# Later scans' inputs in another order over two PSUM banks, and the expert sort in a bank of its own

## The chip, the cores and the metric

The kernel runs on one core of a Trainium2 chip. The core has five engines, each with a queue of its own that it works off in order: PE (TensorE, matrix products; PEld is its weight load), DVE (VectorE), ACT (ScalarE), POOL (GpSimd) and SP (SyncE, which here only starts transfers). They wait for each other by semaphores. PE writes into PSUM[...]. The metric is the device time of one execution in microseconds (us), as the median of several runs; less is better.

## The reference

Two layers over x of 4 batches x 1024 tokens x 128 features. Each layer modulates by a conditioning vector, normalises, mixes tokens, and then applies a routed mixture of experts:

```python
h = layernorm(x) * (1 + ca) + sa
x = x + ga * L0_attention(h)          # 16 heads, 4 key heads, rotary, causal
h = layernorm(x) * (1 + cb) + sb
x = x + gb * L0_ffn(h)                # 8 experts, two best of each token, gated by silu
h = layernorm(x) * (1 + ca) + sa
x = x + ga * L1_mamba(h)              # convolution, selective scan with 16 states
h = layernorm(x) * (1 + cb) + sb
x = x + gb * L1_moe(h)                # 8 experts with a capacity, two best of each token
```

The selective scan is, for every feature and state, h = exp(delta * A) * h + delta * B * u along the tokens, with output y = sum over states of h * C, plus D * u; u is silu of a short causal convolution, delta is softplus of a projection of u, B and C are projections of u, and y is multiplied by silu(z).

## The kernel before

**Layer 0.** Attention runs batch by batch in two passes each. Beside it, in single steps that a Python generator yields, run the parts of other batches: `sort_tokens(b)` (L364) routes the tokens of batch b to layer 0's experts, and `Blocks` (L426 on) computes the experts in blocks of 128 rows. Batch 3's sort, its blocks and the return of its rows (`first_returns`) lie in layer 1's scans.

**The sort.** `sort_tokens` normalises (`norm_steps`), transposes (`feature_steps`, `tp`), makes router logits `fpl`, finds the two best experts (`top2_steps`), and counts in one PSUM tile `fpin`, by matrix products, how many earlier tokens go to each expert. `find_blocks` and `f_pos` (L404) read these counts in PSUM. At the end GpSimd starts 16 indirect transfers `blocks_in` (L418), which put the rows in the order of the experts. All its PSUM tiles have the tag "m".

**Layer 1's scans.** A batch has 32 scans: two halves of 512 tokens by 16 chunks of 8 features x 16 states. For each, `scan` (L988) lets PE spread `du` into PSUM (`pu`), DVE multiply it by `bb` (L997), ACT make the decay `da` by exp (L999), DVE run the scan `h` (L1001) and POOL multiply by `cc` (L1005, `hc`). PE sums groups of four `hc` into `py` (`collected`), and after each half `scan_output` gates it (`yh`), projects it (`pw`), gates again (`wide_gated`, L1023) and POOL adds it to x (L1025).

**The inputs of a batch's scans** come from `scan_inputs(b)` (L923): normalised x (`xn`), transposed (`hT`); for each half the convolution (`xc`, L967) and z (`sz`, L970), both with silu; `delta_steps` (L266) projects `pd`, copies it to `sp_r` and runs softplus (`sp_e` with exp on ACT, then the chain of L249 to L263 on DVE); `spread_delta` makes `dg` (L933) from it; `made_of` (L925) makes `dt` by ones x `dg`, and `bb` and `cc` by projections of `xc`, each in a PSUM bank of 512 columns that ACT copies out (L928). `du` (L977) is the product of `dt` and `xc` on POOL. The inputs of batch 0 (b == 0) use the two banks "m" and "d"; those of the later ones only "m".

**PSUM in layer 1:** four banks for `pu`, one for `py`, one "g" (in the scans of batch 1 used by the first layer's blocks), one "m", and one "d" (for `pw` and the routing `dispatch`).

**What sets the order.** The loop over batches (L1275 on) takes steps of the generators after each pair of scans: in batch 0 the return of layer 0's rows, the sort of batch 3 (four steps a pair), `shift_and_scale` and the inputs of batch 1 (two steps a pair); in later ones `dispatch` of the batch before and the inputs of the next. This program order isn't the order on the chip: a planner at build time puts each instruction into its engine's queue when its operands and its buffer come free by the planner's own reckoning, earlier program order first. A tile that waits for a bank thus moves back in its queue, and others move ahead of it.

Of the kernel before, what the change touches and what calls it, by code (L numbers as in the profile page):

```python
# [11 lines left out]
F32 = mybir.dt.float32  # L12
# [6 lines left out]
P = 128  # L19
# [30 lines left out]
def adaln_two_layers(ctx: ExitStack, tc: tile.TileContext, I: dict, out: bass.AP):  # L50
# [14 lines left out]
    def load(pool, name, eng=nc.sync):  # L65
# [6 lines left out]
    make_identity(nc, ident)  # L72
    ones = cst.tile([P, P], F32, name="ones")
    nc.gpsimd.memset(ones, 1.0)

    causal = cst.tile([P, P], F32, name="causal")
    nc.gpsimd.memset(causal, 0.0)
    nc.gpsimd.affine_select(
        out=causal, in_=causal, compare_op=ALU.is_ge, fill=NEG, base=0, pattern=[[-1, P]], channel_multiplier=1
    )  # L80

    before = cst.tile([P, P], F32, name="before")
    nc.gpsimd.affine_select(
# [277 lines left out]
        nc.vector.tensor_reduce(which, past, AX.X, ALU.add)  # L361
        return blocks, upto, which

    def sort_tokens(b, kept, pool, ps, hpool, tag, xtag="fxn"):  # L364


        xn = pool.tile([P, TB, D], F32, tag=xtag, bufs=1, name="fxn")
        yield from norm_steps(b * TB, TB, xn)
        hT = hpool.tile([P, S], F32, tag=tag, bufs=1, name="fhT")
        yield from feature_steps(xn, hT, ps, modT[0][:, 4, b : b + 1], modT[0][:, 3, b : b + 1])  # L370
        pl = ps.tile([P, TB, NE], F32, tag="m", name="fpl")
        for t in range(TB):
            mm(nc, pl[:, t, :], hT[:, t * P : (t + 1) * P], f_gate)
        yield
        m1, m2, oh1, oh2 = yield from top2_steps(pl, sm)

        both = sm.tile([P, TB, NE], F32, tag="f_both", bufs=1, name="f_both")
        nc.vector.tensor_add(both, oh1, oh2)
        flat = both.rearrange("p t e -> p (t e)")
        pin = ps.tile([P, TB + 1, NE], F32, tag="m", name="fpin")  # L380
        pinf = pin.rearrange("p t e -> p (t e)")
        mm(nc, pinf[:, : TB * NE], before, flat, stop=False)
        for n in range(1, TB):
            mm(nc, pinf[:, n * NE : TB * NE], ones, flat[:, : (TB - n) * NE], start=False, stop=(n == TB - 1))
        mine = sm.tile([P, NE], F32, tag="f_mine", bufs=1, name="f_mine")
        nc.vector.tensor_reduce(mine, both.rearrange("p t e -> p e t"), AX.X, ALU.add)
        mm(nc, pin[:, TB, :], ones, mine)
        yield
        z = sm.tile([P, TB], F32, tag="f_z", bufs=1, name="f_z")
        nc.vector.scalar_tensor_tensor(z, m1, 1e-20, m2, ALU.add, ALU.add)  # L390
        nc.vector.reciprocal(z, z)
        w = keep.tile([P, 2, TB], F32, tag=f"f_w{b}", name="f_w")
        nc.vector.tensor_mul(w[:, 0], m1, z)
        nc.vector.tensor_mul(w[:, 1], m2, z)
        yield

        blocks, upto, which = yield from find_blocks(pin[:, TB, :], NB, sm)
        expert = keep.tile([P, NB], I32, tag=f"f_expert{b}", name="f_expert")
        nc.vector.tensor_scalar(expert, which, float(NE - 1), None, ALU.min)
        yield  # L400

        nc.vector.tensor_tensor(upto, upto, blocks, ALU.subtract)
        pos = sm.tile([P, TB, NE], F32, tag="f_pos", bufs=1, name="f_pos")
        nc.vector.scalar_tensor_tensor(  # L404
            pos, upto.unsqueeze(1).to_broadcast([P, TB, NE]), float(P), pin[:, :TB, :], ALU.mult, ALU.add
        )
        yield
        place = sm.tile([P, 2, TB], F32, tag="f_place", bufs=1, name="f_place")
        placei = keep.tile([P, 2, TB], I32, tag=f"f_placei{b}", name="f_placei")
        for k, oh in enumerate((oh1, oh2)):  # L410
            nc.vector.tensor_mul(oh, oh, pos)
            nc.vector.tensor_reduce(place[:, k], oh, AX.X, ALU.add)
            yield
        nc.vector.tensor_copy(placei, place)
        kept[b] = expert, placei, w
        for t in range(TB):
            for k in range(2):
                nc.gpsimd.indirect_dma_start(  # L418
                    out=f_in[b][:, :],
                    out_offset=bass.IndirectOffsetOnAxis(ap=placei[:, k, t : t + 1], axis=0),  # L420
                    in_=xn[:, t, :],
                    in_offset=None,
                )
                yield
# [71 lines left out]
    with ExitStack() as es:  # L496
# [21 lines left out]


        MW = 512 + QG  # L520
        mask = aw.tile([P, MW], F32, name="mask")
        nc.gpsimd.memset(mask, 0.0)
        for j in range(4):
# [329 lines left out]
    with ExitStack() as es:  # L853
# [68 lines left out]

        def scan_inputs(b):  # L923

            def made_of(g, to, w, of):  # L925
                bank = ps_m.tile([P, 512], F32, tag=next(tags), name="p1")
                mm(nc, bank, w, of)
                nc.scalar.copy(to[:, half_of(g)], bank)  # L928

# [8 lines left out]
            dt, du, bb, cc = (wide(name) for name in ("dt", "du", "bb", "cc"))  # L938
            if b == 0:
                xc, sz, dl = first_made  # L940
                tags = itertools.cycle(("m", "d"))
                dg = spread_delta(dl)

                for g in range(2):
                    tok = half_of(g)
                    made_of(g, dt, ones, dg[g])
                    nc.gpsimd.tensor_mul(du[:, tok], dt[:, tok], xc[:, tok])
                    made_of(g, bb, m_B, xc[:, tok])
                    made_of(g, cc, m_C, xc[:, tok])
                return sz, xc, dt, du, bb, cc  # L950
            tags = itertools.repeat("m")
            xn = mb.tile([P, TB, D], F32, tag="xn", bufs=1, name="xn")
            yield from norm_steps(b * TB, TB, xn)
            hT = wide("hT", 1, S + 3)
# [6 lines left out]
                xc, sz = wide("xc", 1), wide("sz", 1)  # L961
            for g in range(2):
                tok = half_of(g)
                p1 = ps_m.tile([P, 512], F32, tag="m", name="p1")
                for k in range(4):
                    mm(nc, p1, conv_in[:, k, :], hT[:, tok.start + k : tok.stop + k], start=(k == 0), stop=(k == 3))
                nc.scalar.activation(xc[:, tok], p1, AF.Silu, bias=m_cb)  # L967
                p2 = ps_m.tile([P, 512], F32, tag="m", name="p2")
                mm(nc, p2, m_in[:, D:], hT[:, tok.start + 3 : tok.stop + 3])
                nc.scalar.activation(sz[:, tok], p2, AF.Silu)  # L970
                yield
            dl = yield from delta_steps(xc, ps_m)
            dg = spread_delta(dl)
            yield
            for g in range(2):
                made_of(g, dt, ones, dg[g])
            nc.gpsimd.tensor_mul(du, dt, xc)  # L977
            yield

            for to, w in ((bb, m_B), (cc, m_C)):  # L980
                for g in range(2):
                    made_of(g, to, w, xc[:, half_of(g)])
                yield
            return sz, xc, dt, du, bb, cc

        turn = itertools.count()
# [288 lines left out]
        for b in range(B):  # L1275
# [2 lines left out]
            beside, among = [], []  # L1278
            if b == 0:
                beside.append(Beside(first_returns(B - 2, db, 6), 4, 1))  # L1280
                beside.append(Beside(sort_tokens(B - 1, kept, db, ps_m, db, "hT2", "hx"), 2, 4))
                beside.append(Beside(shift_and_scale(), NCH - 3, 1))
            if b == 1:
                among.append(Beside(first_blocks(B - 1), 1, 1))
# [238 lines left out]
```

## Time and profile before

| | |
|---|---|
| median of 3 runs | 2082.4 us (2079.97 to 2082.79) |
| the profiled execution | 2072.22 us |
| its span, first to last instruction | 2070.5 us |
| PE busy | 1779.8 us (86%) |
| DVE busy | 1331.4 us (64%) |
| ACT busy | 944.8 us (46%) |
| POOL busy | 1000.4 us (48%) |
| scans of batch 0 | 1415.1 to 1499.3 us |
| scans of batch 1 | 1530.8 to 1627.4 us |
| scans of batch 2 | 1634.9 to 1742.9 us |
| scans of batch 3 | 1771.0 to 1848.5 us |
| first matrix product of layer 1's experts | 1884.2 us |

The profile is of one execution. A row of its timeline gives start, length, engine, line of the kernel, operation, the tile written and the tiles read, their shapes, and in square brackets how long the engine was idle before and what ended that. `hc<-h,cc` means that `hc` is made of `h` and `cc`. A share of busy time over the whole span mixes attention, scans and experts, which have different limits, so it is read by stretches.

### The profile page before, as it was taken

How to read it: one execution, taken by the hardware profiler on the slowest of the kernel's cores; microseconds unless marked ns; L12 is line 12 of the kernel's file. 1: busy time of each engine (PE TensorE's matmuls, PEld its weight loads, DVE VectorE, ACT ScalarE, POOL GpSimd, SP SyncE). 2: the span in 40 equal slices, each digit the busy share in tenths (PEclk: the TensorE clock that was granted, in tenths of full speed). 3: DMA queues.
4: the chain of work that ended last, by engine and by line, in shares of the span. 5: the costliest groups of instructions: out<-in, count | busy, mean ns of one | idle time of the engine just before them, and what ended most of it. 6: DMA issues, size and time to landing. Idle time of an engine off the chain costs nothing. (4 is left out here: it accounts for less than half of the span.)

```text
span 2070.5 us, 29042 instructions
## 1 busy us (share of the span) xinstructions
PE 1779.8 (86%) x8957; PEld 964.2 (47%) x8957; DVE 1331.4 (64%) x4005; ACT 944.8 (46%) x2071; POOL 1000.4 (48%) x1282
## 2 busy tenths in 40 slices
PE   5999899898999899899989899997779757757994
PEld 2444454453555345455535445553335423325774
DVE  5666556665667666566766566567858887782144
ACT  2364453743455374355455445455556345422321
POOL 3345335446333634633363653227654775773145
PEclk8899999999999999999999999998879887967997
DMA  6502002002222201212210122111003230002255
GB/s 202 186 1 52 1 1 52 1 26 63 64 64 78 56 1 32 78 54 71 78 40 1 48 68 68 51 43 38 31 27 111 76 108 13 8 20 83 80 156 177
DMA packets 104332, 124.63 MB, mean 60 GB/s; under 512 B 15088, under 2 KB 68720, under 8 KB 104176
## 3 DMA queue, kind: packets, MB, share of 16 engines
q1 hardware_dynamic: 83872, 98.75, 15.9%
q0 software_dynamic: 8192, 16.74, 2.7%
q10 hardware_dynamic: 12112, 7.29, 1.2%
q8 instruction: 71, 1.16, 0.2%
q14 instruction: 85, 0.70, 0.1%
HBM read 68.38 MB, written 33.42 MB: 49 GB/s over the span
## 5 line engine op out<-in xcount | busy, mean ns | idle before, releaser
L663 POOL TENSOR_SCALAR pr<-pr,den 128x32 f32<-128x32 f32 (+31 forms) x512 | 356.2, 711 | 308.2 <-DVE den L660 300.2
L657 ACT ACTIVATE pr<-pr,nb 128x32 f32<-128x32 f32 (+31 forms) x512 | 371.7, 727 | 164.5 <-DVE nb L644 158.5
L672 PE MATMUL pt<-ident,pr 128*128 128x128 f32 x2304 | 342.2, 283 | 47.2 <-POOL pr L663 37.2
L672 PEld LDWEIGHTS pt<-ident,pr 128*128 128x128 f32 x2304 | 253.9, 142 | 242.5 <-POOL pr L663 78.1
L46 PE MATMUL sc<-k,q 64*128 64x512 f32 (+14 forms) x1536 | 333.6, 527 | 33.6 <-DVE nb L644 25.5
L46 PE MATMUL po<-pT,v 128*64 128x512 f32 x1152 | 342.6, 621 | 2.8 <-DVE pT L676 2.8
L674 ACT COPY pT<-pt 128x512 f32<-128x512 f32 x288 | 167.5, 582 | 353.9 <-PE pt L672 302.5
L644 DVE CUSTOM_DVE_ANT_0 pr<-sc,mask 128x512 f32<-128x512 f32 (+15 forms) x512 | 272.8, 559 | 67.4 <-PE sc L46 57.0
L676 DVE COPY pT<-pt 128x512 f32<-128x512 f32 x288 | 198.2, 688 | 159.4 <-PE pt L672 145.9
L46 PEld LDWEIGHTS sc<-k,q 64*128 64x128 f32 x1536 | 125.4, 195 | 186.9 <-DVE nb L644 88.6
L1005 POOL TENSOR_TENSOR hc<-h,cc 128x512 f32<-128x512 f32 x128 | 161.7, 1276 | 87.7 <-DVE h L1001 32.2
L46 PE MATMUL pu<-du,spread 128*128 128x512 f32 x256 | 149.6, 694 | 54.5 <-DVE h L1001 43.5
L793 POOL MEMSET pr<- 128x288 f32 x128 | 42.4, 340 | 245.8 <-PE pt L672 241.6
L644 DVE CUSTOM_DVE_ANT_0 pr<-sc,mask,nb 128x416 f32<-128x416 f32 (+15 forms) x256 | 120.0, 496 | 7.3 <-PE sc L46 6.2
L999 ACT ACTIVATE da<-dt,negA 128x512 f32<-128x512 f32 x128 | 91.4, 718 | 62.7 <-DVE h L1001 62.3
L46 PEld LDWEIGHTS po<-pT,v 128*64 128x64 f32 x1152 | 68.9, 135 | 84.0 <-issue 41.4
L46 PEld LDWEIGHTS pu<-du,spread 128*128 128x128 f32 x256 | 47.6, 213 | 128.4 <-DVE h L1001 74.6
L1391 POOL DMA_INDIRECT y<-slots_out,slot x56 | 56.6, 1010 | 88.4 <-PE ph L46 52.1
L613 POOL TENSOR_TENSOR q<-rot_u,rot_v 128x512 f32<-128x512 f32 x64 | 81.3, 1272 | 36.4 <-DMA rot_v<-rot_w 35.3
L997 DVE TENSOR_TENSOR pu<-pu,bb 128x512 f32<-128x512 f32 x128 | 85.1, 684 | 18.0 <-PE pu L46 9.2
L657 ACT ACTIVATION_READ_ACCUMULATOR pr<-pr,nb 128x1 f32 x512 | 96.2, 188 | 0.0
L418 POOL DMA_INDIRECT blocks_in<-fxn,f_placei x64 | 64.6, 1009 | 57.3 <-DMA blocks_in<-fxn,f_placei 46.6
(281 smaller groups left out, 2695.3 us busy)
## 6 DMA issues: line engine op xcount, KB each, us to landing
fw<-in_f_w SPq DMA_DIRECT2D x92, 320.0 KB, 2.9
rot_v<-rot_w SPq DMA_DIRECT2D x300, 64.0 KB, 2.0
gw<-in_g_w SPq DMA_DIRECT2D x15, 512.0 KB, 5.7
fxe<-blocks_in SPq DMA_DIRECT2D x28, 192.0 KB, 2.5
blocks_out<-fye SPq DMA_DIRECT2D x28, 192.0 KB, 2.8
blocks_in<-mask SPq DMA_DIRECT2D x20, 256.0 KB, 2.9
slots_in<-mask SPq DMA_DIRECT2D x16, 256.0 KB, 3.7
g_w<-in_g_w SPq DMA_DIRECT2D x8, 512.0 KB, 7.3
```

The costliest lines, as they stand in the source:

```text
L46: return nc.tensor.matmul(out, lhsT, rhs, start=start, stop=stop)
L418: nc.gpsimd.indirect_dma_start(out=f_in[b][:, :], out_offset=bass.IndirectOffsetOnAxis(ap=placei[:, k, t : t + 1], axis=0), in_=xn[:, t, : ...
L613: nc.gpsimd.tensor_add(to, u.rearrange("p (n q) -> p n q", q=QG), v.rearrange("p (n q) -> p n q", q=QG))
L644: nc.vector.tensor_tensor_reduce(out=pr[hp][:, g, lo:hi], in0=sc[:, hp, : hi - lo], in1=mask[:, MW - hi + lo :] if hi == nk else mask[:, : ...
L657: nc.scalar.activation(p, p, AF.Exp, bias=nb[:, last, hp : hp + 1], scale=-1.0, accum_out=den[:, hp : hp + 1])
L663: nc.gpsimd.tensor_scalar(p, p, den[:, hp : hp + 1], 1.0, ALU.mult, ALU.mult)
L672: next_to(hp == 0 and g == 0, lambda: nc.tensor.transpose(to, p, ident))
L674: nc.scalar.copy(pT[:, hp, :], pt)
L676: nc.vector.tensor_copy(pT[:, hp, :], pt)
L997: nc.vector.tensor_mul(pu, pu, bb[:, tok])
L999: nc.scalar.activation(da, dt[:, tok], AF.Exp, scale=negA[:, c : c + 1])
L1005: nc.gpsimd.tensor_mul(hcs[-1], h, cc[:, tok])
```

## The change

- `scan_inputs` of batches 1 to 3 takes banks from `new_bank()`: alternately "m" and "g" for batches 1 and 3, only "m" for batch 2 (whose inputs are made in the scans of batch 1, when "g" holds blocks).
- In it the order is new: both convolutions; then `pd`; then both z; then softplus, with B beside its first part and C beside its second; then `dg`, `dt`, and `du` in two halves.
- The sort of batch 3 uses bank "d" in place of "m". In every sort the counts are copied from PSUM (`f_ahead`), and what follows reads the copy.
- The mask's `causal` pattern is a tile of attention's pool (tag "fam") in place of a constant of its own.

```diff
-    causal = cst.tile([P, P], F32, name="causal")
-    nc.gpsimd.memset(causal, 0.0)
-    nc.gpsimd.affine_select(
-        out=causal, in_=causal, compare_op=ALU.is_ge, fill=NEG, base=0, pattern=[[-1, P]], channel_multiplier=1
-    )
...
-    def sort_tokens(b, kept, pool, ps, hpool, tag, xtag="fxn"):
+    def sort_tokens(b, kept, pool, ps, hpool, tag, xtag="fxn", bank="m"):
...
-        yield from feature_steps(xn, hT, ps, modT[0][:, 4, b : b + 1], modT[0][:, 3, b : b + 1])
-        pl = ps.tile([P, TB, NE], F32, tag="m", name="fpl")
+        yield from feature_steps(xn, hT, ps, modT[0][:, 4, b : b + 1], modT[0][:, 3, b : b + 1], tag=bank)
+        pl = ps.tile([P, TB, NE], F32, tag=bank, name="fpl")
...
-        pin = ps.tile([P, TB + 1, NE], F32, tag="m", name="fpin")
+        pin = ps.tile([P, TB + 1, NE], F32, tag=bank, name="fpin")
...
         mm(nc, pin[:, TB, :], ones, mine)
+        ahead = sm.tile([P, TB + 1, NE], F32, tag="f_ahead", bufs=1, name="f_ahead")
+        nc.vector.tensor_copy(ahead, pin)
...
-        blocks, upto, which = yield from find_blocks(pin[:, TB, :], NB, sm)
+        blocks, upto, which = yield from find_blocks(ahead[:, TB, :], NB, sm)
...
-            pos, upto.unsqueeze(1).to_broadcast([P, TB, NE]), float(P), pin[:, :TB, :], ALU.mult, ALU.add
+            pos, upto.unsqueeze(1).to_broadcast([P, TB, NE]), float(P), ahead[:, :TB, :], ALU.mult, ALU.add
...
+        causal = ab.tile([P, P], F32, tag="fam", name="causal")
+        nc.gpsimd.memset(causal, 0.0)
+        nc.gpsimd.affine_select(
+            out=causal, in_=causal, compare_op=ALU.is_ge, fill=NEG, base=0, pattern=[[-1, P]], channel_multiplier=1
+        )
         mask = aw.tile([P, MW], F32, name="mask")
...
         def scan_inputs(b):
 
+            def new_bank():
+                pool, tag = next(tags)
+                return pool.tile([P, 512], F32, tag=tag, name="p1")
+
             def made_of(g, to, w, of):
-                bank = ps_m.tile([P, 512], F32, tag=next(tags), name="p1")
+                bank = new_bank()
...
-                tags = itertools.cycle(("m", "d"))
+                tags = itertools.cycle(((ps_m, "m"), (ps_m, "d")))
...
-            tags = itertools.repeat("m")
+
+            free = b != 2
+            tags = itertools.cycle(((ps_m, "m"), (ps_g, "g"))) if free else itertools.repeat((ps_m, "m"))
...
             for g in range(2):
                 tok = half_of(g)
-                p1 = ps_m.tile([P, 512], F32, tag="m", name="p1")
+                p1 = new_bank()
                 for k in range(4):
                     mm(nc, p1, conv_in[:, k, :], hT[:, tok.start + k : tok.stop + k], start=(k == 0), stop=(k == 3))
                 nc.scalar.activation(xc[:, tok], p1, AF.Silu, bias=m_cb)
-                p2 = ps_m.tile([P, 512], F32, tag="m", name="p2")
-                mm(nc, p2, m_in[:, D:], hT[:, tok.start + 3 : tok.stop + 3])
-                nc.scalar.activation(sz[:, tok], p2, AF.Silu)
                 yield
-            dl = yield from delta_steps(xc, ps_m)
-            dg = spread_delta(dl)
-            yield
+            delta = delta_steps(xc, ps_m)
+            next(delta)
             for g in range(2):
+                p2 = new_bank()
+                mm(nc, p2, m_in[:, D:], hT[:, g * 512 + 3 : g * 512 + 515])
+                nc.scalar.activation(sz[:, half_of(g)], p2, AF.Silu)
+            yield
+
+            try:
+                next(delta)
+                for g in range(2):
+                    made_of(g, bb, m_B, xc[:, half_of(g)])
+                yield
+                next(delta)
+                for g in range(2):
+                    made_of(g, cc, m_C, xc[:, half_of(g)])
+                yield
+                next(delta)
+                assert False
+            except StopIteration as end:
+                dg = spread_delta(end.value)
+            yield
+            for g in range(2):
+                tok = half_of(g)
                 made_of(g, dt, ones, dg[g])
-            nc.gpsimd.tensor_mul(du, dt, xc)
-            yield
-
-            for to, w in ((bb, m_B), (cc, m_C)):
-                for g in range(2):
-                    made_of(g, to, w, xc[:, half_of(g)])
-                yield
+                nc.gpsimd.tensor_mul(du[:, tok], dt[:, tok], xc[:, tok])
+            yield
             return sz, xc, dt, du, bb, cc
...
-                beside.append(Beside(sort_tokens(B - 1, kept, db, ps_m, db, "hT2", "hx"), 2, 4))
+                beside.append(Beside(sort_tokens(B - 1, kept, db, ps_m, db, "hT2", "hx", "d"), 2, 4))
```

## The prediction

> **What bounds the kernel now.** I read the page first (engine shares, slices, chain of waits), then cut the span into stretches at the starts and ends of the scans (L1001), the work of layer 1 that runs from 1415 to 1848 us. The reason for the cut: before it the slices show PE at 9 tenths in nearly every one, and the change touches next to nothing there; in the scans PE falls to 7 and the chain of waits is made of `DVE h L1001`, `POOL hc L1005` and `issue`. Each batch has 32 scans. The last of one batch and the first of the next bound a gap. The busy times of the stretches, in pairs of batch and gap (length; then busy us and instructions of PE, PEld, DVE, ACT, POOL; PE's granted clock; DMA share; GB/s):
>
> ```profile
> 1415.00:1499.30 84.30, 65.90 (x200) 27.14 (x198) 73.55 (x133) 46.26 (x84) 58.27 (x54) 0.84 0.08 26
> 1499.30:1530.80 31.50, 17.69 (x46) 7.93 (x47) 9.39 (x57) 14.46 (x24) 15.04 (x15) 0.57 0.06 19
> 1530.80:1627.40 96.60, 84.91 (x414) 48.08 (x412) 86.81 (x181) 55.96 (x105) 50.87 (x45) 0.98 0.27 81
> 1627.40:1634.90 7.50, 6.11 (x17) 3.56 (x18) 1.95 (x7) 1.28 (x2) 6.84 (x7) 0.60 0.12 33
> 1634.90:1742.90 108.00, 75.81 (x288) 35.63 (x286) 92.23 (x184) 48.12 (x92) 76.18 (x64) 0.83 0.22 75
> 1742.90:1771.00 28.10, 17.40 (x70) 10.08 (x71) 10.90 (x53) 14.03 (x25) 21.70 (x19) 0.74 0.11 33
> 1771.00:1848.50 77.50, 54.60 (x164) 18.47 (x162) 73.87 (x116) 30.34 (x59) 57.54 (x48) 0.83 0.04 12
> ```
>
> Inside a batch DVE is busy 85 to 95%: it bounds. In the three gaps (31.5 + 7.5 + 28.1 = 67.1 us) no engine is full: DVE does 9.4, 2.0 and 10.9 us. There a chain of dependences sets the time. The timeline of the first gap shows the chain:
>
> ```profile
> 1501.95 1.01 POOL L418 DMA_INDIRECT blocks_in<-fxn,f_placei  x1 [0.70 <-issue]
> 1502.99 1.27 POOL L1005 TENSOR_TENSOR hc<-h,cc 128x512 f32<-128x512 f32 x1
> 1504.32 1.93 PE L46 MATMUL py<-hc,gather 128*32 128x512 f32 x8 [6.37 <-POOL hc L1005]
> 1506.18 2.08 PE L46 MATMUL p<-hT,m_in_sb 128*128 128x512 f32 x2
> 1509.76 2.18 PE L46 MATMUL pd<-m_dt_sb,xc 128*128 128x1 f32 x16
> 1519.99 2.05 PE L46 MATMUL p<-dg,ones 128*128 128x512 f32 x2 [7.09 <-DVE dg L933]
> 1525.49 2.35 POOL L977 TENSOR_TENSOR du<-dt,xc 128x1024 f32<-128x1024 f32 x1 [4.79 <-ACT dt L928]
> 1530.81 1.22 DVE L1001 TENSOR_TENSOR_SCAN h<-da,pu 128x512 f32<-128x512 f32 x1
> ```
>
> The second z matrix and `pd` stand in PE's queue behind `py`, which waits for the last products `hc` on POOL, and those stand behind issues of `blocks_in`. Then softplus, `dg`, both `dt` and a `du` over both halves follow one after another through the one bank m.
>
> **The change, part by part.** The instructions' order of the changed kernel is known from its build, so I count in it.
>
> *Gap 0 to 1.* The sort of batch 3 no longer holds m, so `xn`, the convolutions, `pd`, B, C and `dt` all stand before the 29th scan of batch 0 in PE's and ACT's queues, both halves of `du` before hc 27 on POOL. Between the batches DVE has no instruction but pu (56 others before). Gap 31.5 to about 1.
>
> *Gap 1 to 2* (m only). `du` stands before the last two products, B and C are copied ahead; 6 other DVE instructions are left. 7.5 to about 2.
>
> *Gap 2 to 3.* Softplus still ends after the last scan; 27 DVE instructions against 52. POOL issues six `slots_in`, adds a gated x and only then makes `du`:
>
> ```profile
> 1744.68 1.02 POOL L1088 DMA_INDIRECT slots_in<-hs,desti  x1 [0.31 <-DVE rank L1083]
> 1746.02 1.00 POOL L1088 DMA_INDIRECT slots_in<-hs,desti  x1 [0.30 <-issue]
> 1747.32 0.97 POOL L1088 DMA_INDIRECT slots_in<-hs,desti  x1 [0.30 <-DMA slots_in<-hs,desti]
> ```
>
> The pitch is 1.29. POOL's leg: last hc 1.3 + 6 x 1.29 + x 1.3 + half of `du` 1.2 (2.35/2) + pu matmul 1.1 + pu product 0.7 = 13.3; I take 13.8 with semaphores. The other leg (hc 1.3, py 1.1, yh, nine softplus steps, `dg` 1.22, `dt` matmul and copy) ends near 9 and is hidden. Gain 14.3; bounds 8 and 18.
>
> Sum of the gaps: -30.5 - 5.5 - 14.3 = -50.3.
>
> *What comes back.* **DVE instructions that lay in a gap now lie among scans.** Counted by batch (all but pu and scan): 68, 117, 119, 51 before; 87, 144, 142, 55 after: 73 more, among them the softplus of batches 1 and 3 and layernorm statistics. In the first gap one cost 9.39/57 = 0.165 us. Beside `hc` on POOL it can cost more, as two steps of the same form in batch 1 show:
>
> ```profile
> 1607.54 1.19 DVE L257 SCALAR_TENSOR_TENSOR sp_s<-sp_s,sp_w 128x8 f32<-128x8 f32 x1
> 1609.25 0.15 DVE L257 SCALAR_TENSOR_TENSOR sp_s<-sp_s,sp_w 128x8 f32<-128x8 f32 x1
> ```
>
> The first began inside an `hc` (1607.43 to 1608.70). The Trainium skill, "SBUF — State Buffer", section "Who interferes with whom", gives a rule that speaks against this change: a DVE instruction with two SBUF inputs and a GpSimd one that reads SBUF share a port pair under an exclusive lock, and the later one blocks until the earlier ends. How often does it strike? Of the 359 such other instructions in the four batches, 34 lasted over 0.4 us longer than the shortest of their form, 35.1 us in all: 9.5%, 1.03 us each. So one costs 0.165 + 0.098 = 0.263, and 73 cost 19 us. If the lock struck each of them: 73 x 1.2 = 88 us. I take the measured share; bounds 12 and 45.
>
> **POOL.** The 16 `blocks_in` issues of batch 3's sort, ten of which lay in the gap, now lie between hc 19 of batch 0 and hc 6 of batch 1. An issue takes 0.98 and waits for the landing of the one before; alternating with one hc the pitch was 3.0 (1498.94, 1501.95). I laid out the queue: 16 issues, 18 hc, two halves of `du`, two adds of x, eight copies of `scb`: 53 us from about 1475 to 1528. DVE alone would be there at about 1520. Scans may run three buffers of `h` ahead of POOL, so 0 to 8 us; I take 5.
>
> **ACT.** Six table loads now stand within three scans (after `da` 21, 22 and 23) and `pu` 20 waits in PE's queue behind the first `pd`, which waits for ACT's first `xc`; scan 21 waits behind `sp_r` for the second.
>
> ```profile
> 1488.01 1.28 ACT L967 ACT_TABLE_LOAD   x1
> 1489.30 0.69 ACT L967 ACTIVATE xc<-p,m_cb_sb 128x512 f32<-128x512 f32 x1
> ```
>
> By the row six are 6 x 1.29 = 7.7 us. "ScalarE: Activation LUTs", "What ACT_TABLE_LOAD costs", adds a drain and says about 2.66 us a switch: 16 us. The trace shows no drain (`da` ended at 1488.0, and `xc` began 1.29 later). Three `da` ahead hide most; 3 us by the row, 11 by the page. The number of table loads is unchanged (56), and DMA traffic too.
>
> **Tail.** Eight `slots_in` of batch 2 stand behind the last hc instead of one. Six lie beside the DVE chain of the last routing; two (2.6) and both `hs` (2.5) then stand before the last eight issues, the first experts' rows wait for these, and PE's experts wait for the rows. One issue less counts for the first load: +4; bounds 0 and 9.
>
> **At no cost.** Each of the four sorts gains one DVE copy (128x72, about 0.2 by its neighbours): three lie in attention where PE is at 9 tenths; without that cover, 0.6 us. The mask built from another buffer comes before the first scores need it; attention's order is otherwise swapped in a few places: 0, give or take 3. In the gaps matmuls ran at half clock (pairs of 2.05 against 1.02); that goes with the gaps and is counted there.
>
> Sum: -50.3 + 19 + 5 + 3 + 4 = -19.3. The profiled execution took 2072.2 (span 2070.5), so it becomes 2053. It lay 10 us under the median of the runs shown; from 2082.4 I get **2063**.
>
> **Rivals.** *A, hidden better:* moved instructions at 12, POOL 0, ACT 0, tail 0, the third gap at 10: -42, 2041. For it: ACT and POOL are busy only 30 to 70% in a batch. Against: DVE is at 85 to 95%, moved work isn't free. *B, POOL takes over:* it stays behind into batch 1 and costs 8 more, and the third gap is 5 longer: -6, 2076. For it: POOL is busy 58 of 84 us before the 16 issues come. *C, slower, the port lock:* without any blocked instruction the sum is -50.3 + 12 + 12 = -26; each blocked one costs 1.03, so from 25 of the 73 (34%) on the change loses. At half, 37, it is +12: 2094. Against: 9.5% measured. For: the moved ones stand in runs (sort, softplus) where POOL is now fuller. *D, nothing:* waits merely change places, 2082. The order speaks against it.
>
> **How the numbers follow.** Likeliest 0.58 (own range 2050 to 2074), A 0.14, B 0.14, C 0.09, D 0.05. A measurement of this kernel tells 0.2% (4 us) from no change. Faster: 0.58 + 0.14 + most of B = 0.83; same 0.07; slower 0.10. Range 2041 to 2080: it takes in A's value and B, leaves C and D out.
>
> **What would show it.** First gap under 3 us, second under 4, third 10 to 20 with `du` behind `slots_in`; batch 1 about 6 us longer; few DVE instructions of 1.2 us among the moved ones; first expert matmul 3 to 6 us later after the last scan. It is wrong if batches 0 to 2 grow by more than 45 us together, or if attention moves by more than 3.

## The result, and the profile after

The changed kernel takes **2096.06 us** (median of five executions, 2092.72 to 2101.17) against 2082.79 us (2079.97 to 2086.09) for the kernel before on the same chip. The ratio is 1.006, with a 95% interval of 1.0041 to 1.0079: the change costs 13 us, where the prediction said that it gains 19.

Its first profiled execution has a span of 2094.9 us. The same stretches as before the change, cut at the first and last scan (L1021 now) of each batch; columns: window, length, then busy us and instructions of PE, PEld, DVE, ACT, POOL, granted clock of PE, DMA share, GB/s:

```profile
1412.70:1511.40 98.70, 76.94 (x249) 33.88 (x249) 82.07 (x152) 53.20 (x97) 67.99 (x68) 0.84 0.08 25
1511.40:1512.10 0.70, 0.70 (x3) 0.22 (x3) 0.56 (x2) 0.69 (x1) 0.70 (x1) 1.00 0.00 0
1512.10:1626.10 114.00, 92.58 (x403) 48.66 (x401) 98.00 (x208) 62.71 (x116) 56.60 (x45) 0.91 0.21 61
1626.10:1628.90 2.80, 2.38 (x14) 1.66 (x15) 2.80 (x8) 1.49 (x3) 1.28 (x1) 1.00 0.78 209
1628.90:1758.10 129.20, 85.96 (x318) 41.08 (x317) 98.54 (x208) 51.61 (x97) 86.43 (x75) 0.80 0.21 72
1758.10:1775.30 17.20, 10.65 (x31) 4.47 (x32) 8.09 (x28) 6.24 (x11) 14.85 (x14) 0.80 0.09 35
1775.30:1855.20 79.90, 56.65 (x180) 21.17 (x178) 71.92 (x119) 33.66 (x67) 54.46 (x44) 0.83 0.02 6
```

The gaps are as forecast: 0.7, 2.8 and 17.2 us in place of 31.5, 7.5 and 28.1. The batches are not: 98.7, 114.0 and 129.2 us in place of 84.3, 96.6 and 108.0. In batches 0 and 2, PE and POOL grew most: PE from 65.9 to 76.9 and from 75.8 to 86.0 us, POOL from 58.3 to 68.0 and from 76.2 to 86.4; DVE grew by 8.5 and 6.3. In batches 1 and 2 the granted clock of PE is a little lower than before (0.91 for 0.98, 0.80 for 0.83); what that adds was not tried by itself.

The end of batch 0 in the timeline (POOL and the scans only) shows that the first chain was in fact moved ahead:

```profile
1497.45 1.28 POOL L1002 TENSOR_TENSOR du<-dt,xc 128x512 f32<-128x512 f32 x1
...
1499.90 1.28 POOL L1002 TENSOR_TENSOR du<-dt,xc 128x512 f32<-128x512 f32 x1
...
1507.65 1.02 POOL L414 DMA_INDIRECT blocks_in<-fxn,f_placei  x1 [0.15 <-issue]
...
1511.37 1.00 POOL L414 DMA_INDIRECT blocks_in<-fxn,f_placei  x1 [0.17 <-issue]
...
1512.10 1.22 DVE L1021 TENSOR_TENSOR_SCAN h<-da,pu 128x512 f32<-128x512 f32 x1
```

Both halves of `du` are there 11 us before batch 1 begins, and `blocks_in` now stands between the products. In the third gap `du` comes, as forecast, behind `slots_in` and an add of x:

```profile
1761.46 1.29 POOL L1025 TENSOR_TENSOR hc<-h,cc 128x512 f32<-128x512 f32 x1
...
1764.22 0.98 POOL L1108 DMA_INDIRECT slots_in<-hs,desti  x1 [0.30 <-issue]
...
1769.73 0.98 POOL L1108 DMA_INDIRECT slots_in<-hs,desti  x1 [0.30 <-issue]
...
1770.72 1.29 POOL L1045 TENSOR_TENSOR x<-x,wide_gated 128x512 f32<-128x512 f32 x1
...
1771.94 1.28 POOL L1002 TENSOR_TENSOR du<-dt,xc 128x512 f32<-128x512 f32 x1
```

**What stops the scans in batch 2.** The longest wait of DVE inside a batch (timeline of batch 2; the wait and its releaser are in the brackets):

```profile
1656.62 0.98 POOL L1108 DMA_INDIRECT slots_in<-hs,desti  x1 [0.84 <-DMA slots_in<-hs,desti]
1657.59 1.31 POOL L1025 TENSOR_TENSOR hc<-h,cc 128x512 f32<-128x512 f32 x1
1659.06 1.00 POOL L1108 DMA_INDIRECT slots_in<-hs,desti  x1 [0.17 <-issue]
1660.08 1.28 POOL L1025 TENSOR_TENSOR hc<-h,cc 128x512 f32<-128x512 f32 x1
...
1661.42 1.94 PE L46 MATMUL py<-hc,gather 128*32 128x512 f32 x8 [7.35 <-POOL hc L1025]
...
1663.29 0.80 PE L46 MATMUL pf<-fw,rest 128*128 128x128 f32 x2
...
1664.55 0.29 DVE L479 TENSOR_TENSOR fye<-pf,gate 128x128 f32<-128x128 f32 x1 [8.18 <-PE pf L46]
1664.76 1.21 DVE L1021 TENSOR_TENSOR_SCAN h<-da,pu 128x512 f32<-128x512 f32 x1
```

Read from below: the scan stands behind `fye` on DVE, `fye` waits for `pf`, `pf` stands behind `py` on PE, and `py` waits for a product `hc` that stands behind issues of `slots_in` on POOL. From 1629.2 to 1661.5 all 16 issues of a dispatch stand there, and POOL makes eight products in that time. In the kernel before, DVE has no wait of this kind in batch 2; its two largest there are (columns: us in total, times, longest):

```profile
DVE x L311 <- DMA fy<-blocks_out,f_placei: 8.7, 9, 2.4
DVE ln_st L142 <- POOL x L1025: 2.0, 1, 2.0
```

Batch 0 has a chain of the same shape without an issue right ahead of it. Its longest wait of DVE for `pu` is 3.60 us:

```profile
1503.55 0.52 POOL L877 COPY scb<-silu_c 128x128 f32<-128x128 f32 x2
1503.88 0.72 PE L46 MATMUL rp<-wrow,scb 128*128 128x128 f32 x4 [3.04 <-POOL scb L877]
1504.44 1.84 PE L46 MATMUL pu<-du,spread 128*128 128x512 f32 x2
...
1506.32 0.70 DVE L1017 TENSOR_TENSOR pu<-pu,bb 128x512 f32<-128x512 f32 x1 [3.60 <-PE pu L46]
```

Here PE's next `pu` stands behind `rp`, and `rp` waits for small copies (`scb`) that POOL makes only after both halves of `du`, an issue and two products.

**What makes one DVE instruction last 8 us.** A second place in batch 2:

```profile
1701.91 1.28 POOL L1025 TENSOR_TENSOR hc<-h,cc 128x512 f32<-128x512 f32 x1
1702.22 8.00 DVE L305 SCALAR_TENSOR_TENSOR x<-fy,f_w,x 128x128 f32<-128x128 f32 x1 [0.23 <-DMA fy<-blocks_out,f_placei]
...
1703.14 2.35 POOL L1056 TENSOR_TENSOR hs<-hx,row_scale 128x1024 f32<-128x1024 f32 x1
1705.43 2.34 POOL L1118 TENSOR_TENSOR x<-x,gate_bias 128x1024 f32<-128x1024 f32 x1
1707.73 2.34 POOL L1057 TENSOR_TENSOR hs<-hs,row_shift 128x1024 f32<-128x1024 f32 x1
...
1710.69 1.24 DVE L1021 TENSOR_TENSOR_SCAN h<-da,carry,pu 128x512 f32<-128x512 f32 x1
```

It began 0.31 us after a product on POOL and ended 0.15 us after POOL had done that product and three more instructions; its median in the scans is 0.34.

Counted over batches 0 to 2 on DVE, from the traces of the first profiles ("others" are the instructions that begin inside a batch, all but `pu` and the scans, with the sum of their lengths; "blocked" means over 0.4 us longer than the shortest of the same operation and shape, and the us are the excess; the expectations below were written from another count of the idle time, 61 for 63.3):

| batches 0 to 2 | before | after |
|---|---|---|
| others: instructions, us | 307, 103.9 | 376, 133.2 |
| of these blocked: instructions, us | 24, 22.5 | 30, 36.7 |
| DVE idle, us | 36.3 | 63.3 |

POOL's issues by stretch (b: batch, g: gap):

| | b0 | g01 | b1 | g12 | b2 | g23 | b3 |
|---|---|---|---|---|---|---|---|
| `blocks_in` before / after | 6 / 10 | 9 / 1 | 1 / 5 | | | | |
| `slots_in` before / after | | | 3 / 0 | 3 / 0 | 10 / 22 | 15 / 9 | 14 / 8 |

Of the issues, 27 lay in the gaps before, ten after.

### The profile page after: what moved, and what is told of

Its sections match the earlier page's. It is cut to its first block, busy times and chain, and to the rows that moved or that the text cites. A ratio compares the mean times of both kernels' runs of the same rounds, so it can differ in the third digit from the quotient of the medians.

```text
span 2094.9 us, 29046 instructions
## 1 busy us (share of the span) xinstructions
PE 1787.4 (85%) x8957; PEld 964.9 (46%) x8957; DVE 1343.1 (64%) x4009; ACT 945.4 (45%) x2071; POOL 1001.9 (48%) x1285
## 5 line engine op out<-in xcount | busy, mean ns | idle before, releaser
L46 PE MATMUL pu<-du,spread 128*128 128x512 f32 x256 | 155.3, 715 | 69.5 <-DVE h L1021 53.3
L646 DVE CUSTOM_DVE_ANT_0 pr<-sc,mask,nb 128x416 f32<-128x416 f32 (+15 forms) x256 | 119.8, 496 | 10.4 <-PE sc L46 9.7
L1019 ACT ACTIVATE da<-dt,negA 128x512 f32<-128x512 f32 x128 | 91.2, 718 | 73.1 <-DVE h L1021 71.8
L46 PEld LDWEIGHTS po<-pT,v 128*64 128x64 f32 x1152 | 69.4, 136 | 84.6 <-issue 43.3
L1411 POOL DMA_INDIRECT y<-slots_out,slot x56 | 56.6, 1010 | 96.8 <-PE ph L46 52.1
```

What stands on the lines that cost most here:

```text
L46: return nc.tensor.matmul(out, lhsT, rhs, start=start, stop=stop)
L646: nc.vector.tensor_tensor_reduce(out=pr[hp][:, g, lo:hi], in0=sc[:, hp, : hi - lo], in1=mask[:, MW - hi + lo :] if hi == nk else mask[:, : ...
L1019: nc.scalar.activation(da, dt[:, tok], AF.Exp, scale=negA[:, c : c + 1])
```

## The experiments

The theories changed on the way. At first: T, what leaves a gap comes back among the scans, against R, the scans gain and the tail loses. Then, to find what of the scans: P (POOL's queue), L (the port lock of the prediction), D (the moved DVE instructions and the waits for their inputs, whatever POOL does). Last, within P: S (the `slots_in` carry the loss) and K (the `blocks_in` carry it). The profiles of the experiments are one for each kernel. Times between chips differ by 15 us, so a ratio is always to the kernel before on the same chip. Stretches in us:

| kernel | b0 | g01 | b1 | g12 | b2 | g23 | b3 | first to last scan | ratio (95%) |
|---|---|---|---|---|---|---|---|---|---|
| before_again | 84.1 | 31.4 | 96.8 | 6.6 | 108.6 | 29.9 | 76.8 | 434.2 | |
| after_again | 100.9 | 0.7 | 115.0 | 2.8 | 128.2 | 17.3 | 79.1 | 444.0 | |
| sort_own | 91.7 | 13.9 | 98.4 | 15.6 | 123.2 | 28.3 | 77.2 | 448.3 | 1.0076 (1.0049 to 1.0103) |
| inputs_only | 91.7 | 10.0 | 115.8 | 0.0 | 130.9 | 6.9 | 84.6 | 439.9 | 1.0050 (1.0030 to 1.0069) |
| before_ni | 83.5 | 27.5 | 105.9 | 5.8 | 99.7 | 21.8 | 79.9 | 424.1 | |
| after_ni | 97.9 | 1.2 | 120.4 | 1.0 | 104.8 | 9.4 | 81.6 | 416.1 | |
| before_nh | 75.3 | 35.2 | 94.3 | 1.1 | 106.5 | 27.9 | 67.7 | 407.9 | |
| after_nh | 87.4 | 1.1 | 98.5 | 3.9 | 113.9 | 15.4 | 70.1 | 390.3 | |
| before_ns | 84.2 | 31.4 | 99.2 | 2.1 | 104.9 | 27.6 | 71.8 | 421.0 | |
| after_ns | 99.1 | 0.7 | 113.4 | 2.8 | 116.7 | 11.6 | 81.8 | 426.2 | |
| b1_only | 91.7 | 10.0 | 117.6 | 11.4 | 114.5 | 20.9 | 79.0 | 445.0 | 1.0032 (1.0015 to 1.0049) |
| b13_own | 99.5 | 0.7 | 107.6 | 17.1 | 124.1 | 7.0 | 83.3 | 439.3 | 1.0067 (1.0044 to 1.0090) |
| as_24 | 100.4 | 0.7 | 109.3 | 4.6 | 120.7 | 11.7 | 80.8 | 428.2 | 0.9992 (0.9974 to 1.0010) |
| bs_24 | 92.2 | 9.6 | 106.2 | 1.6 | 127.3 | 26.4 | 83.9 | 447.1 | 1.0054 (1.0034 to 1.0075) |
| as24_s15 | 103.6 | 1.1 | 111.4 | 5.0 | 120.0 | 11.7 | 80.8 | 433.7 | 1.0002 (0.9983 to 1.0021) |
| as_14 | 100.7 | 1.3 | 106.8 | 12.1 | 113.6 | 15.0 | 81.5 | 431.1 | 0.9983 (0.9965 to 1.0001) |

### Both kernels once more: before_again, after_again

No edit; second profiles, to learn what of the 24 us between the first two belongs to the change.

> The kernel before, unchanged, for a second profile. The first profiled execution lay 10 us under the median. If the 24 us between the two first profiles are partly chance (theory T: 13 of them are the change, lost inside batches 0 to 2; the rest is how long the last weight loads take), this execution takes 2079 to 2087, its scans (start of the first to end of the last) stay at 433 us within 3, and the time from the last first-layer matmul of the experts to the end is longer than the 69.5 of the first profile by 5 to 12. If the tail is the change's own cost (rival R), it stays at 69 to 72.

> The kernel after, unchanged, for a second profile. T: the batches repeat at 99, 114, 129 and 80 us within 3 each, because the order on each engine is fixed, the 8.0 us instruction in batch 2 included; the last stretch lies between 70 and 82. R: the last stretch stays at 79 to 82. If the 8.0 us instruction was a chance event, batch 2 is 7 us shorter.

Measured: spans of 2071.6 and 2086.5 us, 14.9 apart. The scans repeat within 2.2 us per stretch (434.2 and 444.0 from first to last), the 8.0 us instruction too (7.97). The last stretch, from the last first-layer matmul of the experts to the end, was 69.0 and 68.1 us before, 79.9 and 68.2 after. So ten of the 24 us were not the change. In the other kernels below that stretch lay at 68.2 to 70.5 us six times and at 76.7 to 83.5 eight times; it went with the occasion on which they ran, not with the kernel. R fell: the tail loses only the 3.9 us up to the first expert matmul (35.5 to 39.4). T's guesses that the before kernel's tail would be longer and that the after kernel's would be 70 us or more (68.2) were misses; that the batches repeat was right.

### One half of the change each: sort_own, inputs_only

sort_own is the kernel before with the sort's bank and the copy of its counts (and the mask's tile in its new place); inputs_only the kernel after with

```diff
-    def sort_tokens(b, kept, pool, ps, hpool, tag, xtag="fxn", bank="m"):
+    def sort_tokens(b, kept, pool, ps, hpool, tag, xtag="fxn"):
...
-        ahead = sm.tile([P, TB + 1, NE], F32, tag="f_ahead", bufs=1, name="f_ahead")
-        nc.vector.tensor_copy(ahead, pin)
...
-                beside.append(Beside(sort_tokens(B - 1, kept, db, ps_m, db, "hT2", "hx", "d"), 2, 4))
+                beside.append(Beside(sort_tokens(B - 1, kept, db, ps_m, db, "hT2", "hx"), 2, 4))
```

> The kernel before with the sorting half alone: batch 3's sort in bank d with its counts copied, the old order of the scans' inputs in bank m. T (what leaves a gap comes back among the scans, about 1.1 us for each us): the first gap falls from 31 to 5 to 15 us, batch 0 grows by 10 to 20, the other batches and gaps stay; 2076 to 2088. R (the scans gain and the tail loses, and the tail's loss comes with the inputs of batch 3): the first gap's gain is kept, 2055 to 2068.

> The kernel after with the sort put back in bank m without the copy: the new order of the scans' inputs alone, two banks for batches 1 and 3. T: the first gap stays at 20 to 30, batch 0 as before; batches 1 and 2 grow by 10 to 20 each as in the kernel after, the third gap falls to 17; 2086 to 2100. R: the scans gain 14 to 20, the tail takes 10 to 14 back; 2074 to 2082.

Both halves lose by themselves, 0.76% and 0.50%, so their sum is twice what the whole loses (0.6%). In sort_own the first gap fell as T expects (31 to 14 us), but batch 0 grew by less (8 us for 10 to 20), and T said that the other batches stay: batch 2 with its gap to batch 1 grew by 24 us, although nothing in it was edited. The planner had ordered it otherwise (16 `slots_in` in batch 2, ten before; 135 other DVE instructions for 121). inputs_only was a miss for both: T had the first gap stay at 20 to 30 us and batch 0 as before (10.0 and 91.7 came, so the new order of the inputs closes most of that gap by itself, without the sort's bank), and R had the scans gain 14 to 20 us (they lost 6). In it 30 `slots_in` stand in batch 2, which is the longest of all (130.9). This pointed to POOL.

### Less work for POOL: before_ni, after_ni, before_nh, after_nh

In the two kernels "ni" the scattering issues are not made (of `blocks_in` those of batch 3):

```diff
-                nc.gpsimd.indirect_dma_start(
-                    out=f_in[b][:, :],
+                if b < B - 1:
+                    nc.gpsimd.indirect_dma_start(
+                        out=f_in[b][:, :],
...
-                    nc.gpsimd.indirect_dma_start(
-                        out=xd[k][:, :],
...
+                    pass
```

In "nh" a product has 64 columns:

```diff
-                nc.gpsimd.tensor_mul(hcs[-1], h, cc[:, tok])
+                nc.gpsimd.tensor_mul(hcs[-1][:, :64], h[:, :64], cc[:, tok.start : tok.start + 64])
...
+                part = hc[:, :64].unsqueeze(1).to_broadcast([P, 8, 64])
```

> The kernel before without two groups of GpSimd issues: the 16 blocks_in of batch 3's sort and the slots_in of the dispatches beside the scans. Left out of the computation: the rows that these issues would scatter (the experts then read zeros). Scans before: 434 us from the first to the last. Theory P (POOL's queue: products hc stand behind issues, PE's py behind hc, DVE behind PE): the gaps shrink, since the last hc of a batch no longer waits; 405 to 420. Theory D (DVE itself: moved instructions cost their time, and it waits in order for their inputs): 415 to 428.

> The kernel after without the same issues. Scans after: 443 us, 9.5 more than before. What counts is the difference to the kernel before without them. P: without the issues the change gains over the scans, 10 us or more. D: the difference stays at +3 to +15, and in batches 0 to 2 DVE is still idle 50 us or more (61 now).

> The kernel before with products hc of 64 columns in place of 512, which PE reads eight times; left out of the computation: the other 448 columns. POOL then has about 0.2 us per scan in place of 1.28, and all issues stay. Theory L (the port lock: DVE instructions with two SBUF inputs blocked by hc, 22 us in batches 0 to 2): other DVE instructions of batches 0 to 2 fall from 104 to about 85 us; scans 410 to 420. P: POOL has room for its issues, the gaps shrink too. D: scans 425 to 434.

> The kernel after with products of 64 columns. L: other DVE instructions fall from 133 to about 97 us, and the difference to the kernel before, treated alike, turns from +9.5 to -5 or below. P: it turns too, since POOL is no longer behind; DVE's idle time in batches 0 to 2 falls from 61 to 40 or less. D: the difference stays at +5 to +12, with DVE idle for 55 or more.

The sign turns in both pairs. Without the issues the change gains 8.0 us over the scans (424.1 to 416.1) where it loses 9.4 with them (mean of the two profiles of each); with short products it gains 17.6 (407.9 to 390.3). D fell: it had the difference stay at +3 to +15. Both pairs change more than what was left out, though, because the planner ordered the queues anew: compared by operation and tiles, of the 722 DVE instructions of the scans only 274 stand in the same order in before_ni as in the kernel before (450 in before_nh), and of the 717 of the kernel after 378 in after_ni (627 in after_nh). The stretches of batch 2, without the issues, before and after the change:

```profile
1633.00:1732.80 99.80, 75.17 (x247) 32.07 (x246) 88.37 (x169) 51.45 (x90) 63.93 (x52) 0.79 0.16 55
```

```profile
1627.40:1732.20 104.80, 76.54 (x260) 32.90 (x258) 91.25 (x185) 50.09 (x92) 64.42 (x53) 0.80 0.15 54
```

Batch 2 grows by 5 us there, by 21 with the issues. With short products, before and after:

```profile
1616.70:1723.20 106.50, 78.14 (x299) 35.91 (x297) 89.76 (x195) 50.26 (x94) 50.06 (x68) 0.82 0.25 79
```

```profile
1604.50:1718.40 113.90, 82.40 (x330) 40.21 (x328) 91.89 (x212) 52.28 (x98) 59.17 (x76) 0.84 0.26 87
```

The two pairs take different parts of the loss away. Growth from before to after over batches 0 to 2 (the row without `slots_in` is from the next section):

| | other DVE instructions, us | DVE idle, us |
|---|---|---|
| as they are | +29.3 (103.9 to 133.2) | +27.0 (36.3 to 63.3) |
| without `slots_in` | +26.6 (105.9 to 132.5) | +16.9 (33.7 to 50.6) |
| without the issues | +29.9 (103.3 to 133.2) | +7.7 (36.0 to 43.7) |
| with short products | +11.8 (92.2 to 104.0) | +14.6 (34.4 to 49.0) |

The idle time is P's part: 19 of its 27 us go with the issues. The longer instructions are L's: 17.5 of 29.3 us go with the products, most of it blocked time, whose growth falls from 14.2 us (22.5 to 36.7) to 0.3 (10.4 to 10.7), with 4 and 5 blocked instructions for 24 and 30. L had expected the others at 85 and 97 us and measured 92.2 and 104.0; its limit of -5 was passed, and its forecast of 410 to 420 for the kernel before was too high (407.9). P was right in the sign and wrong in four levels: the kernel before without issues lies in D's range (424.1; P said 405 to 420), the gain without issues is 8.0 where P said 10 or more, DVE's idle time with short products is 49.0 where P said 40 or less, and the gaps of before_nh shrink by only 3 us (67.1 to 64.2).

### Which issues: before_ns, after_ns

The same without `slots_in` alone.

> The kernel before without the slots_in issues of the dispatches beside the scans (left out of the computation: the rows that they scatter); blocks_in stays. Scans 434 before, 424 without both groups. S: 424 to 429. K: 430 to 434.

> The kernel after without the slots_in issues, blocks_in kept; scans 443 as it is, 416 without both groups. S: 414 to 421, that is less than the kernel before without them. K: 430 to 440, still more than the kernel before without them.

This pair changes little else: all 717 DVE instructions of after_ns stand in the same order as in the kernel after, 696 of 722 in before_ns as in the kernel before. The change still loses 5.2 us over the scans (421.0 to 426.2), so the `slots_in` carry 4.2 of the 9.4. But that sum hides two things that go against each other. Batches 0 to 2 grow by 40.9 us in place of 53.1, and DVE's idle time there by 16.9 in place of 27.0: 12 and 10 us go with the `slots_in`. Batch 3, on the other hand, gains 5.7 us without them before the change (77.5 to 71.8) and loses 2.0 after it (79.8 to 81.8). K had the sign; the levels fit neither (421.0 is below what both named, 426.2 lies between them). The 8.2 us wait of `fye` is gone in after_ns (batch 2: 116.7 for 129.2), but batches 0 and 1 keep most of their growth. What the `blocks_in` carry is left open: it shows only as the difference to the pair without both, whose order is another.

### The new inputs for some batches only: b1_only, b13_own

```diff
+        def scan_inputs(b):
+            return (inputs_new if b in (0, 1) else inputs_old)(b)
```

(for b13_own `(0, 1, 3)`, with the sort in its own bank; in b1_only it is in bank m, and the mask's tile is the new one).

> The kernel before with the new order of inputs and two banks for batch 1 alone; sort in bank m, batches 2 and 3 in the old order. Theory P (what left the gaps was POOL's queue and port at work, and costs as much or more among scans): batch 0 with its gap falls by 14 as in the kernel after; the issues of blocks_in still run into batch 1, and batches 1 and 2 with their gaps lose 5 to 15 of it; 2070 to 2084 against 2083 on the first chip, that is -10 to +2. Theory D (each batch pays for its own moved inputs): batches 1 and 2 stay as before, -12 to -16.

> The kernel after with batch 2's inputs in the old order and bank m alone. D: batch 1 returns from 114 to 97 us, its gap to 7; 10 to 14 us less than the kernel after, the same as before within 4. P: what POOL has to issue stays, so batch 1 and 2 keep at least half of their growth; 2 to 8 us less than the kernel after.

b1_only: batch 0 and its gap fall by 14 us (115.5 to 101.7), as both theories had it; then batch 1 and its gap give back 26 (103.4 to 129.0), with nothing edited in the inputs that are made in it. It is 0.32% slower, 6.7 us: above P's range (-10 to +2) and farther from D's. b13_own: batch 1 comes down half the way (107.6 for 115, D said 97), its gap grows from 2.8 to 17.1, and the kernel takes as long as the whole change. Both theories expected some gain and there is none. Undoing the change batch by batch doesn't undo the loss. The issues get another place each time (7 `slots_in` in the gap to batch 2 and 23 in batch 2 of b13_own); that this is the reason was not tried.

### Another pace of the dispatches: as_24, bs_24

as_24 is the kernel after with

```diff
-                sending = Beside(dispatch(b, 0, TB), 2, 3)
+                sending = Beside(dispatch(b, 0, TB), 2, 4)
```

and a step for each issue in place of one for two. The routing steps of a dispatch thus come sooner and its issues are spread thinner; the inputs are not edited. bs_24 is b1_only with the same edit.

> The kernel after with its dispatches taken four steps for each pair of scans in place of three, and each slots_in issue a step of its own. Nothing else moves. P: four of batch 0's slots_in come to stand in batch 1 and no longer in the first half of batch 2, where a wait of 8.2 us for a product behind issues stops DVE: that wait goes, batch 2 falls by 5 to 10, 4 to 10 less than the kernel after. D: within 4 of the kernel after.

> The kernel with the new order for batch 1 alone, with the same pace of the dispatches. P: 3 to 10 less than with the old pace, and faster than before by 5 to 20. D: within 4 of it.

as_24 takes the whole loss away: 0.9992 of before (0.9974 to 1.0010), 15 us less over the scans than the kernel after (443.2 to 428.2), more than P said. It does so with more other DVE work in batches 0 to 2 (391 instructions, 138.0 us) and less idle time (47.0 us for 63.3). Six `slots_in` now stand in batch 1 and 17 in batch 2 (0 and 22 after the change). What DVE waited for in batch 2 (columns: us in total, times, longest), first in the kernel after, then in as_24:

```profile
DVE fye L479 <- PE pf L46: 8.2, 1, 8.2
DVE x L305 <- DMA fy<-blocks_out,f_placei: 7.4, 7, 3.5
DVE ln_st L136 <- POOL x L1045: 5.7, 3, 3.4
```

```profile
DVE x L305 <- DMA fy<-blocks_out,f_placei: 7.7, 6, 3.6
DVE ln_st L136 <- POOL x L1045: 3.7, 2, 3.5
```

The `fye` wait is gone; the wait for the gathered rows is nearly as long (7.7 for 7.4). The edit moved more than POOL's issues: 457 of 717 DVE instructions keep their order. So as_24 shows that the order decides, and the trace that the wait behind the issues is one part of it. bs_24 is a miss for P: no gain (1.0054 for 1.0032). Its trace shows the same chain in another place: batch 2 stays long (127.3) with an 8.8 us wait of DVE's `ln_st` for an add of x on POOL, which first issues five more `slots_in` and makes a product. So the pace isn't good in itself; it helps or not by where it puts the issues and what goes with them.

### Two more places: as24_s15, as_14

as24_s15 is as_24 with batch 3's sort at `1, 5` in place of `2, 4`; as_14 is the kernel after with dispatches at `1, 4` and a step for each issue.

> The kernel after with dispatches at four steps for each pair of scans, and batch 3's sort begun one pair earlier with five steps for each pair in place of four, so that its 16 blocks_in begin some two products earlier. S: within 3 of the same without the earlier sort, which took as much as the kernel before (ratio 0.9992). K: 4 to 8 less, ratio 0.995 to 0.998.

> The kernel after with dispatches at four steps for each pair and begun one pair earlier, so that batch 0's slots_in begin 8 in batch 1 in place of 6 and end sooner in batch 2. S: 2 to 6 less than with the later begin, ratio to before 0.996 to 0.999. K: within 2 of it.

as24_s15 did not do what it was made for: the first `blocks_in` came 63.1 us after the first scan, 61.4 in as_24. It tells nothing about K. as_14 has eight `slots_in` in batch 1 and 11 in batch 2, which falls to 113.6 us; it is the fastest of those with the change, 0.9983 of before, and its interval (0.9965 to 1.0001) still touches one. S said a ratio of 0.996 to 0.999, K within 2 us of as_24, whose ratio differs by 0.0009 (some 2 us), so the run doesn't tell the two apart. No version was shown to beat both kernels. Whether that pace helps the kernel before as well was not tried, so as_14 says nothing for or against the change.

## Why the prediction was wrong

Step by step, with the second profiles of both kernels (14.9 us apart in the span):

| step | forecast | measured |
|---|---|---|
| three gaps | -50.3 | -47.1 (67.9 to 20.8) |
| batches 0 to 2: DVE 19, POOL 5, ACT 3 | +27 | +54.6 (289.5 to 344.1) |
| batch 3 | in the 19 | +2.3 |
| last scan to first expert matmul | +4 | +3.9 |
| attention, to the first scan | 0, give or take 3 | +0.8 |
| experts and end | 0 | +0.5 |
| sum | -19.3 | +15.0 |

**The gaps** were right in mechanism and nearly in size; the second gap (-3.8 for -5.5) and the third (-12.6 for -14.3) gave a little less. The third is 17.3 us where 13.8 was forecast, because the sum lets the last product follow the last scan at once: two issues and another product stood before it, and it ended 4.7 us after the scan in place of 1.3. **The tail** and **attention** were right.

Batches 0 to 2 grew by 53.1 us in the first profiles (288.8 to 341.9). DVE's records have 29.3 of longer and added instructions, 10.1 of idle time that goes with the `slots_in` and 16.9 of other idle time (56.3 in all, because records of neighbours overlap by some us). Forecast were 19, 5 and 3.

**The step that failed is POOL's:** "Scans may run three buffers of `h` ahead of POOL, so 0 to 8 us; I take 5." Its layout of the queue was right: the 16 `blocks_in` took 54.3 us from the first to the last where it said 53, and products in batch 1 began at most 2.9 us after their scans, so the three buffers were never used up there. Two other things are wrong in it. It costs the queue by what waits for POOL through the buffers of `h`, and the trace shows another way: PE's `py` waits for `hc`, whatever stands behind `py` in PE's queue waits with it (`pf`, the next `pu`), and DVE waits for these in order. The copies `scb`, which the layout lists, delay DVE in the same way. And it counts the `blocks_in` only. The `slots_in` of the dispatches appear in the working for the third gap and the tail, but not inside the batches, where they moved as well: ten in batch 2 before, 22 after. At the pitch of 1.29 that the prediction itself reads, these twelve alone are 15.5 us of POOL's time in a batch in which POOL was busy for 76 of 108. The pair without `slots_in`, with DVE's order nearly kept, prices them: batches 0 to 2 grow by 12.2 us less. So this part alone, put at nothing, is more than the 5 taken for the whole and outside its bounds of 0 and 8. Without both groups of issues batches 0 to 2 grow by 19 us less (34.0) and the scans as a whole turn from +9.4 to -8.0, but there the order changed too, so that the share of the `blocks_in` and of the new order stays open.

**The DVE step was right in kind and too small in size:** forecast 19 for the four batches, measured 24.6, which is 29.3 in batches 0 to 2 less 4.7 in batch 3 (24.9 to 20.2). Its count held: 69 more instructions in batches 0 to 2 and four in batch 3 are the 73 forecast. So did its share, with 8.0% of all blocked in batches 0 to 2 (9.5% was taken). What failed is the price of a blocked one, 1.22 us (36.7/30) for 1.03, and the price of one that is not: (133.2 - 36.7)/376 = 0.257 us. The 0.165 is the mean of the first gap, the cheapest of the three; the third gap had 10.90/53 = 0.206. The one instruction of 8.00 us is more than half of the growth in blocked time (14.2).

**ACT** was not tried by itself. In the kernel after no wait of DVE for ACT in batches 0 to 2 is longer than 1.3 us. DVE waited 6.9 us for PE's `pu` in batch 0 (1.1 before), and the longest part of that, 3.60, goes back to POOL's `scb` as shown above; what ACT adds to the rest stays open.

**The rivals.** B, POOL takes over, named the mechanism and priced it at 8 more in one place; it left the sum at -6 because it looked at batch 1 alone. C, the lock, needed a third of the moved instructions to be blocked; that did not happen (six more blocked, 69 more instructions), and yet with short products, which take away blocked time and load of POOL together, the change gains 17.6 us over the scans. The two were priced one at a time, each on top of a sum that held without the other. A's value is a slip of rounding: 2082.4 less 42 is 2040, just outside the range given. The prediction's own test of failure, batches 0 to 2 more than 45 us longer, is what came (53.1 and 54.6).

## What to carry to other kernels

A gap between two stages is not empty because no engine is full in it: list what every queue works off there, above all the queue with the most work in the stages beside it, and count those instructions where they land when the gap closes. In-order engines hand a delay on: cost an engine that falls behind by following what stands behind its consumer's wait on the next queue, not by the buffers between them alone. And where a planner sets the order, the pieces of a change are not additive, and leaving work out to price it can order everything else anew: look where the unedited instructions came to stand, and trust most the pair whose order stayed.

## What was not expected of the hardware

The Trainium skill, "SBUF — State Buffer", section "Who interferes with whom", has the later instruction wait until the earlier one ends. Here the waiting DVE instruction was not let in between POOL's instructions either: 8.00 us through a product and three more. An instruction of the same form took 7.96 to 8.02 us in seven more profiles (after_again, sort_own, inputs_only, after_ns, as_24, as24_s15, as_14), and 5.62, 8.95 and 9.08 in b1_only, b13_own and bs_24. With products of 64 columns it took 7.05 and, in after_nh, 7.01, three times 2.34. Each time it ended 0.15 or 0.16 us after the last of three to five POOL products or adds in a row. The kernel before has none, but as_24 and as_14, which lose nothing, have one, so it doesn't decide the loss. Scans (one input in SBUF, one in PSUM) took 1.19 to 1.28 us in the kernel after, although 60 of them ran beside a product `hc` for 47.5 us in all.
